# A four-layer graph network in one planned program: another start for graphs 0 to 2, and half-wise normalisation in the first and last graph

## The chip, the cores and the metric

One NeuronCore of one Trainium2 chip runs the whole program. The metric is the device time of one execution in microseconds (us). Engines: PE multiplies matrices (PEld is its weight load, which overlaps), DVE works on vectors, ACT evaluates functions, POOL does reductions over partitions and issues the adjacency loads, SP issues the other DMAs. Each engine runs its own queue strictly in order; an instruction whose input is not there holds up everything behind it on that engine.

## The reference

Sixteen graphs of 1024 nodes with 128 features pass four layers. Each layer adds its input and normalises each row (mean 0, variance 1):

```python
x = _layernorm(x + gat(x, adj, W0, a0))            # layer 0: one head, relu
x = _layernorm(x + gat8(x, adj, adj, W1, a1))      # layer 1: 8 heads of 16, elu
x = _layernorm(x + rgcn(x, adj, rel_w, self_w, ..))# layer 2: mean over neighbours, own layernorm, relu
x = _layernorm(x + attn4(x, adj, W3))              # layer 3: 4 heads of 32, masked softmax
```

The adjacency matrix holds 0 and 1 (about 3% ones). In layers 0 and 1 the logit of a pair is leaky_relu(s_i + t_j), so its exponential factors: per source j and head the kernel needs max(R_i, q_j) times the mask, where R is a row over all target nodes, the same on all 128 partitions, and q_j one number per partition.

## The kernel before

**Tiling.** 1024 nodes are 8 blocks of 128. Work is in transposed form: source nodes on partitions, target nodes along the row. In the line numbers of the profile:

- `before0` (L597): loads adjacency `m` (eight 128x1024 tiles, cast to fp8 by POOL's DMA, L605), the transposed features `xT` (L621), multiplies them with W0 joined with the two attention vectors and a mean column (`products`, L393), copies the result to `hd` and `mean` (L629, L636), takes the maximum of the target terms (L643, then all-reduce L416), and makes r, q and the scaling of hd (L654 to L681). The row R0 over all partitions: for graph 0 by eight products of r, broadcast, with the identity (L585, into PSUM); for the others by a transpose (L498), a copy (L500), a write of 8x128 to DRAM (L503) and a load that repeats it on all partitions (L672).
- `layer0` (L687): per half of the targets and per j one DVE instruction of 128x512 makes z (L697), PE adds four products of 129 columns to two accumulators (L709); then L741, L730, the residual L750 and the normalisation.
- `before1`, `layer1` (L755, L839): as layer 0, with eight heads: 64 DVE instructions of 128x1024 a graph (L849), each with eight narrow PE products (L857). For graph 0 the first four rows come by products with the identity (L585, copied by ACT, L810), all others through DRAM (L814).
- `last1` (L915), `layer2` (L937): elu and residual (L920, L924, L929), sums (L423), normalisation; then products with the weights, split in three bf16 parts (L952 to L975), 192 PE products with the mask (L989), means (L1010), normalisation, gamma and beta (L1026, L1033), relu and residual (L1040), sums, normalisation.
- `before3`, `layer3` (L1050, L1119 on): heads, their norms (L1104) and the bound `low` (L1111); then per half and j: the squared mask gap by ACT (L1129), scores by PE (L1139 for the mask, L1150), the exponential by ACT (L1221), values and totals by PE (L1165, or L1176 and L1187 in the last two graphs, where DVE adds pairs first, L1243), and the tail L1255 to L1288. The last graph is normalised half by half at this point already.
- `layernorm` (L427): DVE offsets (L438 or L442), eight ACT squares with sums (L448), Ln and Exp (L461, L466), five small DVE instructions (L470 to L480), eight ACT applications (L486). Its argument `half` restricts it to four blocks.

**What sets the order.** Every operation is a `step` with an engine, an expected duration, a due time and what it reads and writes. `Plan.run` (L168) emits steps one at a time: for each engine it finds the earliest possible start by its own expected times and the free buffers, and among the steps within a small `WINDOW` of it the one with the earliest due time. So the due times (the many constants added to `due` and `at`) decide the order within each engine, and the program that results is fixed. `plan.user` gives users of a scarce pool turns. The waits in the program come from the instructions' real operands, not from what a step is said to read. After graph 2 or 3 the order is periodic: layer 3 of one graph runs beside layers 0, 1 and 2 of the next ones.

**Buffers that matter here:** 9 tiles z, 7 tiles R, two accumulators acc1, two PSUM work areas wk, one tile x0, and two each of x1, x2, x3 (layer outputs).

Of the kernel before, what the change touches and what calls it, by code (L numbers as in the profile page):

```python
# [76 lines left out]
class Plan:  # L77
# [8 lines left out]
    SAME = 43.42  # L86
    WINDOW = {"DVE": 0.32, "ACT": 0.56, "POOL": 24.74, "SP": 1.21, "PE": 0.04}
    URGENT = 87.13
# [79 lines left out]
    def run(self):  # L168
# [18 lines left out]
        while left:  # L187
# [17 lines left out]
            for buf in s.bufs:  # L205
                if buf.place is None:
                    buf.place = min((p for p in self.places[buf.pool] if p.holder is None), key=lambda p: p.free)
                    buf.place.holder = buf
                    if buf.pool in self.turns:
                        self.turns[buf.pool].remove(buf)  # L210
# [23 lines left out]
def tile_binary(  # L234
# [62 lines left out]
    LATER1 = 126.77  # L297
    LATER3 = -19.68
    LATERX = 258.97
# [43 lines left out]
    places("x1", 2, [P, NB, P])  # L343
    places("x2", 2, [P, NB, P])
    places("x3", 2, [P, NB, P])
# [40 lines left out]
    def products(xT, w, due, into, us, floor=0.0):  # L386
# [14 lines left out]
        step("PE", us, due - 42.13, emit, [xT, w], [out], holds=[into], floor=floor)  # L401
        return out, lambda: out.t.rearrange("p (k c) -> p k c", c=SLOT)[:, :, :cols]

    def turned(x_nat, chunk, due):
# [3 lines left out]
            "PE", 0.44, due - 52.2, lambda: transposes(pt.t, [x_nat.t[:, chunk * HB + k, :] for k in range(HB)]),  # L408
            [(x_nat, chunk), xT, identity], [pt],
        )  # L410
        step("ACT", 0.47, due + 19.59, lambda: nc.scalar.copy(xT.t, pt.t[:, :HALF]), [pt], [xT])
        return xT

    def over_partitions(v, op, shape, due, op_us=None):
        got = little(f"all{shape[1]}", shape)
        step("POOL", 0.6 if op_us is None else op_us, due - 256.91, lambda: nc.gpsimd.partition_all_reduce(got.t, v.t, P, op), [v, heated], [got], lag=0.6)  # L416
        return got

    def sums(y, half, tot, due):
# [3 lines left out]
            "DVE", 0.62, due - 13.18, lambda: nc.vector.tensor_reduce(tot.t[:, ks], y.t[:, ks, :], AX.X, ALU.add),  # L423
# [3 lines left out]
    def layernorm(y, tot, due, rest=None, half=None):  # L427
# [16 lines left out]
        step("DVE", 0.1, due - 236.47, minus_mean, [tot_of, rest] if rest else [tot_of], [off])  # L444
# [7 lines left out]
        for pair in pairs:  # L452
            step(
                "ACT", 1.05, due + pair - 6.55, lambda pair=pair: square(pair), [off, (y, pair // 2)], [(squared, pair), junk]
            )
# [4 lines left out]
            "ACT", 0.17, due - 65.07,  # L460
# [4 lines left out]
            "ACT", 0.17, due - 217.77,  # L465
# [3 lines left out]
            "DVE", 0.1, due - 138.7,  # L469
# [12 lines left out]
        step("DVE", 0.35, due - 474.69, newton, [about, var, off], [rstd, shift])  # L482
# [7 lines left out]
        for pair in pairs:  # L490
            step("ACT", 0.77, due + pair - 6.15, lambda pair=pair: apply(pair), [shift, rstd], [(y, pair // 2)])

    def rows_everywhere(r, flat, count, due):
# [4 lines left out]
            "PE", 0.2, due + 269.89, lambda: nc.tensor.transpose(pt.t[: count * NB, :P], flat(r.t), ident), [r, rT, identity], [pt]  # L498
        )
        step("ACT", 0.2, due - 282.01, lambda: nc.scalar.copy(rT.t[: count * NB, :], pt.t[: count * NB, :P]), [pt], [rT])  # L500
        step(
            "SP", 0.5, due - 721.27,
# [7 lines left out]
    def load(due, into, out, in_, part=None):  # L510
        step("SP", 0.45, due - 48.89, lambda: nc.sync.dma_start(out=out(), in_=in_), [], [(into, part)], lag=3.0)

    def constants(due):
        none = Buf("z", "none")
        step("DVE", 0.2, due - 932.32, lambda: nc.vector.memset(none.t[:, :P], 0.0), [], [none])
        for n, (out_, in_) in enumerate(
# [7 lines left out]
                "ACT", 0.1, due - 1208.47,  # L524
                lambda out_=out_, in_=in_: nc.scalar.dma_start(out=out_(), in_=in_()),
                [none] if n == 0 else [square_of] if n == 2 else [], [square_of] if n < 2 else [identity], lag=2.5,
            )
            if n == 0:

                def table():  # L530
                    nc.scalar.preload_act_table_set("natural_log_exp_and_others")
                    nc.scalar.activation(warm, warm, AF.Exp)

                step("ACT", 1.5, due - 840, table, [], [heated])
# [1414 lines left out]
```

## Time and profile before

| | us |
|---|---|
| median of the runs (2182.18 to 2188.67) | 2186.32 |
| the profiled execution | 2186.08 |
| its span | 2184.2 |
| first z of layer 0 (L697) / of layer 1 (L849) | 24.67 / 67.75 |
| graph 0's norms (L1104) / first scores (L1139) | 234.9 / 240.8 |
| last layer 1 sums copied (L887), then `low` of graph 15 (L1111) | 2022.8, 2112.2 |
| last exponential (L1221) ends / last apply (L486) starts | 2167.0 / 2177.0 |

In the profile a group is given as line, engine, operation, output <- inputs; "idle before <- X" is time that the engine stood still ahead of it and what ended that. PE busy is the union of its matmuls as modelled; the granted clock is TensorE's, as a share of full speed. A trace counts a product of f32 operands as two matmuls (x64 rows for 32 products). The page gives busy shares of PE 94%, DVE 89%, ACT 81% over the span.

### The profile page before, as it was taken

The numbers are of one execution on the slowest core, as the hardware profiler recorded it, in microseconds if no ns is written. First come the engines' busy times: TensorE is split into PE (matmuls) and PEld (weight loads), VectorE is DVE, ScalarE is ACT, GpSimd is POOL, SyncE is SP. The second block draws the span as 40 slices with busy tenths as digits, with TensorE's granted clock in tenths as the row PEclk, the third lists the DMA queues.
The fourth block names the chain that finished last, engine by engine and source line by source line (L and its number), as shares of the span: only waits on it lengthen the run. The fifth ranks groups of instructions, "written<-read, shape, count | busy, mean of one in ns | idle before, by whom it ended". The sixth has DMA issues, their size and how long they took to land.

```text
span 2184.2 us, 55248 instructions
## 1 busy us (share of the span) xinstructions
PE 2046.5 (94%) x23344; PEld 982.0 (45%) x23344; DVE 1945.6 (89%) x2883; ACT 1761.7 (81%) x4360; POOL 109.8 (5%) x185
## 2 busy tenths in 40 slices
PE   6757999999999999999999999999999999999877
PEld 5414445453544545354454435345443635442422
DVE  5799999999999999999999999999999999999444
ACT  3414769889797979979797997979799797979987
POOL 1000000000000000000000000000000000000000
PEclk9888999999999999999999999999999999999989
DMA  7140220412323041232204122220413222020000
GB/s 114 49 98 20 65 60 15 101 38 86 43 79 57 18 100 34 86 43 93 44 18 101 33 91 38 93 43 18 101 33 91 38 91 38 2 78 11 11 2 22
DMA packets 81282, 119.97 MB, mean 55 GB/s; under 512 B 7560, under 2 KB 59136, under 8 KB 81024
## 3 DMA queue, kind: packets, MB, share of 16 engines
q1 hardware_dynamic: 62160, 99.43, 13.7%
q0 software_dynamic: 18432, 16.79, 9.5%
q8 instruction: 184, 3.01, 0.6%
q14 instruction: 74, 0.61, 0.1%
q10 hardware_dynamic: 432, 0.13, 0.0%
HBM read 157.61 MB, written 9.04 MB: 76 GB/s over the span
## 4 chain that ended last, share of the span: by engine, by line
PE 47%; DVE 29%; issue 15%; ACT 5%; DMA 2%; POOL 1%; POOLq 0%; SPq 0%; DVEq 0%; ACTq 0%
DVE z L849 18%; PE acc L709 10%; PE acc L1165 10%; PE acc L857 9%; PE wk L1150 6%; PE wk L384 3%; PE wk L393 3%; PE wk L1139 2%; POOL all L416 1%; PE wk L1062 1%; DMA R<-rows 1%; DVE tot L423 1%; PE acc L1176 1%; DVE rest L957 1%; DVE x L964 1%
## 5 line engine op out<-in xcount | busy, mean ns | idle before, releaser
L849 DVE SCALAR_TENSOR_TENSOR z<-R,q,m 128x1024 f32<-128x1024 f32 x1024 | 1248.2, 1278 | 23.0 <-PE acc L857 20.7
L857 PE MATMUL acc<-z,hh 128*32 128x512 f32 x4096 | 516.7, 613 | 59.4 <-DVE z L849 57.0
L1221 ACT ACTIVATE z<-wk,low 128x1024 f32<-128x1024 f32 x448 | 477.8, 1108 | 29.8 <-PE wk L1150 27.5
L1165 PE MATMUL acc<-z,hh 128*32 128x512 f32 x1792 | 454.3, 598 | 1.7 <-ACT z L1221 1.7
L1165 PE MATMUL acc<-z,ones 128*32 128x512 f32 x1792 | 454.3, 598 | 0.0
L448 ACT ACTIVATE junk<-x,off 128x128 f32<-128x128 f32 x640 | 257.1, 402 | 42.8 <-DVE off L442 26.7
L1150 PE MATMUL wk<-whT,turn 32*64 32x512 f32 x3952 | 287.0, 615 | 0.0
L857 PEld LDWEIGHTS acc<-z,hh 128*32 128x32 f32 x4096 | 117.5, 111 | 367.0 <-issue 226.8
L486 ACT ACTIVATE x<-x,shift,rstd 128x128 f32<-128x128 f32 x640 | 264.6, 487 | 6.8 <-DVE shift L480 6.6
L709 PE MATMUL acc<-hd,z 128*128 128x129 f32 x2048 | 252.3, 279 | 8.2 <-DVE z L697 4.3
L709 PEld LDWEIGHTS acc<-hd,z 128*128 128x128 f32 x2048 | 240.7, 194 | 38.4 <-DVE z L697 16.7
L1165 PEld LDWEIGHTS acc<-z,hh 128*32 128x32 f32 x1792 | 89.6, 109 | 213.2 <-issue 181.7
L697 DVE SCALAR_TENSOR_TENSOR z<-R,q,m 128x512 f32<-128x512 f32 x240 | 165.9, 744 | 22.0 <-DMA R<-rows 22.0
L989 PEld LDWEIGHTS <-m 128*128 128x128 fp8e5 x3072 | 178.4, 98 | 14.4 <-issue 14.4
L989 PE MATMUL wk<-y,m 128*128 128x128 bf16 (+1 forms) x2976 | 175.7, 220 | 0.9 <-DVE y L975 0.9
L1129 ACT ACTIVATE gap<-m,neg_one 128x512 bf16<-128x512 fp8e5 x240 | 171.4, 716 | 0.0
L1139 PEld LDWEIGHTS <-far 32*32 32x32 bf16 x4096 | 37.1, 87 | 217.0 <-issue 214.3
L448 ACT ACTIVATION_READ_ACCUMULATOR junk<-x,off 128x1 f32 x640 | 120.8, 189 | 0.0
L1165 PEld LDWEIGHTS acc<-z,ones 128*32 128x32 f32 x1792 | 89.5, 109 | 53.1 <-issue 53.1
L1139 PE MATMUL wk<-gap,far 32*32 32x512 bf16 x3784 | 106.7, 386 | 5.7 <-ACT R L1221 5.4
L605 POOL DMA_DIRECT2D m<-in_adj_dram x128 | 68.4, 539 | 723.6 <-ACT gap L1129 698.3
L660 ACT ACTIVATE r<-r 128x8 f32<-128x8 f32 x16 | 3.3, 208 | 119.7 <-DVE r L654 119.7
(158 smaller groups left out, 2120.7 us busy)
## 6 DMA issues: line engine op xcount, KB each, us to landing
R<-rows SPq DMA_DIRECT2D x139, 512.0 KB
m<-in_adj_dram POOLq DMA_DIRECT2D x128, 128.0 KB, 5.3
xT<-in_xT_dram SPq DMA_DIRECT2D x32, 256.0 KB
x<-in_x_dram SPq DMA_DIRECT2D x16, 512.0 KB
out_dram<-x SPq DMA_DIRECT2D x15, 512.0 KB
rows<-rT SPq DMA_DIRECT2D x16, 32.0 KB
out_dram<-x SPq DMA_DIRECT2D x2, 256.0 KB
z<-in_L_gnn_a_dram SPq DMA_DIRECT2D x2, 128.0 KB
```

What stands on the lines that cost most here:

```text
L448: nc.scalar.activation(junk.t, y.t[:, k, :], AF.Square, bias=off.t[:, k : k + 1], accum_out=squared.t[:, k : k + 1])
L486: nc.scalar.activation(y.t[:, k, :], y.t[:, k, :], AF.Identity, bias=shift.t[:, k : k + 1], scale=rstd.t[:, k : k + 1])
L697: nc.vector.scalar_tensor_tensor(z.t[:, (j % 2) * HALF : (j % 2 + 1) * HALF], in0=R0.t[:, cols], scalar=q.t[:, j : j + 1], in1=m[j].t[:, c ...
L709: nc.tensor.matmul(av[k // 2].t.rearrange("p (k c) -> p k c", k=2)[:, k % 2, : P + 1], lhsT=z.t[:, at : at + P], rhs=hd.t[:, j, : P + 1], ...
L849: nc.vector.scalar_tensor_tensor(z.t, in0=G["R"][h].t, scalar=q.t[:, j, h : h + 1], in1=m[j].t, op0=ALU.max, op1=ALU.mult)
L857: nc.tensor.matmul(av[half].t[32 * c : 32 * c + 32, :], lhsT=hh.t[:, j, at : at + 32], rhs=zs[c].t[:, half * HALF : (half + 1) * HALF], st ...
L989: nc.tensor.matmul(ps.t[:, k * SLOT : k * SLOT + part.stop - part.start], lhsT=m[j].t[:, rows_i], rhs=y2.t[:, j, part], start=j == 0 and n ...
L1129: nc.scalar.activation(gap.t, m[j].t if b == B - 1 else m[j].t[:, cols], AF.Square, bias=neg_one, accum_out=squares[:, at : at + 1], satur ...
L1139: nc.tensor.matmul(sc[h // 2].t[c * 32 : (c + 1) * 32, (h % 2) * HALF : (h % 2 + 1) * HALF], lhsT=far[rows_r, rows_r], rhs=gap.t[rows_r, c ...
L1150: nc.tensor.matmul(sc[h // 2].t[r * 64 : (r + 1) * 64, (h % 2) * HALF : (h % 2 + 1) * HALF], lhsT=turns[j // HB].t[rows_h, j % HB * P + r ...
L1165: nc.tensor.matmul(av[g].t[at : at + 32, :], lhsT=lhsT, rhs=z.t[:, h, :], start=j == 0, stop=j == NB - 1,)
L1221: lambda g=g, sc=sc, zs=zs: nc.scalar.activation(zs[g].t.rearrange("p h n -> p (h n)"), sc[g].t, AF.Exp, bias=low.t, scale=S3),
```

## The change

Seven things, and all due times and planner constants are set anew (not shown; they reorder every queue).

1. Graph 0's row R0 no longer comes by r and the identity. PE multiplies W0's source vector, repeated over 128 columns, with xT: the sum s_i appears on all partitions at once, in PSUM. DVE adds the maximum and clamps (two halves), ACT takes the exponential. R0 is a tile of pool R.
2. The features of graphs 0 and 1 are loaded first (graph 1's into tiles of pool xTc). The three small DMAs that build the identity go from ACT's queue to SP's, behind these; ACT's table load comes first on ACT.
3. Adjacency loads: graph 1's are said to follow the identity (before: graph 0's maximum), graph 2's to follow graph 1's row R0.
4. Graph 2's layer 0 has a start of 50 instead of two periods, so that it stands with graphs 0 and 1 in the order.
5. `last1` and `layer2` of the first and last graph are done in two halves, normalisations, gamma, beta, relu and sums too. Each layernorm in halves has the same ACT squares and applications but two sets of the small instructions.
6. x1, x2 and x3 share one pool of five tiles (before: two each).
7. Graph 0's layer 1 is planned with all four rows of a group there, and the first tiles of pool R have turns.

```diff
+        if b == 0:
+            straight = Buf("wk", "straight")
...
+            xT = Buf("xTc" if b == 1 else "xT0", "xT0")
...
+            if b == 0:
+                step(
+                    "PE", 0.9, -700 + chunk + 225.08,
+                    lambda xT=xT, chunk=chunk: nc.tensor.matmul(
+                        straight.t[:, chunk * HALF : (chunk + 1) * HALF],
+                        lhsT=w0c.t[:, P : P + 1].to_broadcast([P, P]),
+                        rhs=xT.t, start=True, stop=True,
+                    ),
+                    [xT, w0c], [(straight, chunk)],
+                )
...
-            R0 = G["R0"] = Buf("wk", "R0_0")
+            R0 = G["R0"] = Buf("R", "R0_0")
             for half in range(2):
-                step("PE", ..., row_by_products(lambda: r.t, R0, range(half * HB, half * HB + HB)), [r, identity], [(R0, half)])
+                step("DVE", 0.7, ..., tensor_scalar(R0.t[:, cols], straight.t[:, cols], most.t, 0.0, ALU.add, ALU.max), ...)
+                step("ACT", 0.6, ..., activation(R0.t[:, cols], R0.t[:, cols], AF.Exp, scale=-(1.0 - SLOPE)), ...)
...
-        if b == 1:
-            masks(range(NB), due + 40, [G["after"]])
+        if b in (1, 2):
+            masks(range(NB), due + 40, [identity if b == 1 else graphs[1]["R0"]])
...
+    def portions(b):
+        if b in (0, B - 1):
+            return [(half, slice(half * HB, (half + 1) * HB)) for half in range(2)]
+        return [(None, slice(0, NB))]
...
-        layernorm(o, tot, due + 60.03)
+        for part, ks in portions(b):
+            layernorm(o, tot, due + 60.86, half=part)
...
-    places("x1", 2, [P, NB, P])
-    places("x2", 2, [P, NB, P])
-    places("x3", 2, [P, NB, P])
+    places("x", 5, [P, NB, P])
...
-        at0 = 25 if b == 1 else at
+        at0 = 25 if b == 1 else 50 if b == 2 else at
```

## The prediction

> **What bounds the kernel now.** I read the page first (busy shares, then the 40 slices of 54.6 us), then one table of busy time by stage, then the order of time at both ends.
>
> ```profile
> PE 2046.5 (94%) x23344; PEld 982.0 (45%) x23344; DVE 1945.6 (89%) x2883; ACT 1761.7 (81%) x4360; POOL 109.8 (5%) x185
> ...
> PE   6757999999999999999999999999999999999877
> ...
> DVE  5799999999999999999999999999999999999444
> ACT  3414769889797979979797997979799797979987
> ```
>
> From slice 5 to slice 37 PE is full. The stage table gives 592.67 busy us of 600 for 400 to 1000 us, with DVE at 562.39. The middle is PE-bound with 1.2% idle, and the change leaves PE's work as it is. What can move is PE's idle time at the ends: about 76 us before the first layer 3 (240.9), and 21 us between 2018 and 2166.
>
> ```profile
> 24.67:67.75 43.08, 37.63 (x310) 36.65 (x311) 27.80 (x56) 21.25 (x83) 1.84 (x4) 0.96 0.41 64
> 67.75:156.40 88.65, 54.39 (x356) 18.55 (x358) 85.37 (x82) 21.31 (x60) 6.70 (x10) 0.83 0.37 90
> 156.40:234.90 78.50, 58.03 (x502) 39.42 (x501) 73.64 (x114) 42.71 (x129) 0.00 (x0) 0.87 0.05 14
> ...
> 2018.00:2107.00 89.00, 68.22 (x794) 29.75 (x786) 39.72 (x84) 81.64 (x188) 0.82 (x1) 0.92 0.03 7
> 2107.00:2166.00 59.00, 58.52 (x812) 15.21 (x810) 29.33 (x42) 51.73 (x83) 1.17 (x1) 0.94 0.04 11
> ```
>
> Columns: window, length, then busy us of PE, PEld, DVE, ACT, POOL, granted clock, DMA share, GB/s. Five stages, each with its own bound: layer 0 of graphs 0 and 1 is PE's (37.6 of 43); layer 1 is DVE's (85.4 of 88.7, PE waiting); graph 0's layer 2 and the way to its layer 3 are DVE's again; the last graph's chain is ACT's (81.6 of 89); its layer 3 is PE's (58.5 of 59).
>
> **Start, step 1: layer 0 begins earlier.**
>
> ```profile
> 8.71 3.40 PE L393 MATMUL wk<-w0c,xT 128*128 128x131 f32 x16 [8.71 <-DMA xT<-in_xT_dram]
> ...
> 17.10 0.23 DVE L535 TENSOR_SCALAR far<-b_ident 128x128 bf16<-128x128 f32 x1 [9.93 <-DMA b_ident<-square]
> 18.10 0.15 DVE L643 TENSOR_REDUCE top<-hd 128x1 f32<-128x8 f32 x1
> ...
> 22.30 0.22 ACT L660 ACTIVATE r<-r 128x8 f32<-128x8 f32 x1
> ...
> 24.67 6.68 DVE L697 SCALAR_TENSOR_TENSOR z<-wk,q,m 128x512 f32<-128x512 f32 x10 [1.20 <-PE wk L585]
> ```
>
> The projection ends at 12.1, but the maximum (L643) sits on DVE behind L535, which waits for the identity until 17.10; then r waits on ACT behind graph 1's copies (22.30), and L585 builds the row with the identity. In the changed kernel far is later and the row comes from the features: two products of 512 columns (0.57 us each by row L1062, times 1.65, as L393 takes 0.213 us here against 0.13 later): 14.0. The maximum is out at 13.7 (copies 0.8, L643 and all-reduce 0.6), two DVE passes of 0.67 end at 15.3, ACT's two exponentials at 15.9. q then stands on ACT behind the copy of graph 1's mean, about 16.2. First z at **16.4 instead of 24.67**: 8.3 earlier. PE's first L709 comes at 18.4 instead of 25.47, since graph 0's scaling on ACT now stands behind four copies for graph 1.
>
> Queues it is moved past. The identity's three DMAs go from ACT's queue to SP's, behind four feature loads: start 3.5 instead of 1.35, so landing about 19.3 instead of 17.1. Behind them on SP wait the constants, x0 and graph 1's row. On PE the transpose of graph 1's r, third in layer 0, waits for the identity: 0 to 1.5 us. Graph 1's row landed at 38.17; now its values are ready at 20.5, SP reaches them near 23, and 3.9 of bounce and the 8.3 that L672 took from issue (29.85) bring it to about 36; PE's first use is at 38. Adj: "gated" only orders POOL's queue, the chip waits for nothing new there; graph 2's eight loads go behind graph 1's. Twelve loads and the features kept DMA full from 18.6 to 38.8, some 1.6 us a load, so eight more end near 51, before their use at 57.
>
> **Step 2: graph 2's layer 0 moves in.** PE's order now has three graphs before the first layer 1: 192 products of L709 at 7.41/32 = 0.232 us make 44.5; 32 of L585 7.2; the projections of graph 2 2.1 and w1c's for two graphs 4.1; transposes 2.3; the rest 0.6. That is 60.8, and at the present share of gaps in this stage (5.5 in 43) 69.3. PE starts layer 1 at 18.4+69.3 = **87.7**; it was at about 72. DVE, nine z buffers ahead, has by then done 48 z of layer 0 and nine of layer 1.
>
> **Step 3: DVE from there to graph 0's norms (L1104).** By its order it has 96 z of layer 1 left (1.205 us pitch, 115.7) and 30 us of small work, 145.6; it idles 6 of 167 us in these two stages now, so 151.6: norms at 239.3, before 234.9. In front of it lie, against before, 2 z (2.4), graph 2's head work (2.1) and graph 0's halves: four more sets of L470 to L480 (0.85 each, 3.4) and small change. PE, however, has done 4.1 us more by then (graph 2's transposes 1.0, w1c products 2.1, two z 1.0). Start: 4.4 later, 4.1 less to do: **nil**. The ends: with layer 0 as dense as its best half (7.41 busy of 7.55) norms come at 234, gain 5; with another 4 us of waits at 243, loss 4. I take a gain of 1, near the middle. The 8.3 us are not lost, but graph 2's layer 0 only changes places: it filled 12.6 us of DVE at 212 to 236 before.
>
> **A rule against step 2.** PE's granted clock in the layer 1 stage is 0.83 with PE busy 54.39 of 88.65, so at full clock 45.1. The Trainium skill (TensorE: Matmul & The Clock Gate, "The HAM clock gate") says that an idle window of about 3.4 us drops the array to half clock. If the thinner stage ran wholly at half clock, its 45.1 would be 90, over DVE's 85.4, and PE would bind there: about 5 us worse; the trace shows 0.83 at 61% load, so I do not add it.
>
> **Tail.**
>
> ```profile
> 2057.11 0.69 DVE L975 TENSOR_TENSOR y<-rest,y 128x512 bf16<-128x512 f32 x1 [0.28 <-ACT y L970]
> ...
> 2082.67 1.22 DVE L1026 TENSOR_TENSOR x<-x,b_gamma_bc 128x1024 f32<-128x1024 f32 x1 [4.31 <-ACT x L486]
> ...
> 2112.21 0.15 DVE L1111 TENSOR_SCALAR low<-all 128x1 f32<-128x1 f32 x1 [0.24 <-POOL all L416]
> ```
>
> DVE idles 4.31 us while ACT normalises all eight blocks, although four would do to go on. From the copies of the last layer 1 sums (2022.76) to low, the point from which graph 15's scores may start, it is 89.5 us. In the new ACT order that stretch loses one 0.71 us and five 1.14 us adjacency squares (moved behind it) and gains two exponentials (1.0 each) and three Ln/Exp pairs (0.5 each): 2.9 us less. Of the 7.4 us in which ACT idles I count 4.4 as filled: 2.46 before the xTc copy at 2048.8, then 1.22, 0.6 and part of the small ones, as the second half's squares stand there now. Low is **7.3 earlier**. The deferred squares less the exponentials, 4.4 us, go into the next stage, where ACT has 59-51.7 = 7.3 free but PE has none: I charge 1.5 (0 to 4.4). Tail: gain **5.8**; ends 0 (nothing filled, all repaid in waits) and 9.
>
> Splitting costs: five DVE passes of 128x1024 (1.22) become ten of 128x512 (0.69), 0.8 us by durations, nil by pitch (1.25 against 0.61). VectorE: DVE Perf Modes, in its errata section, names a fixed cost for each instruction and advises tiles of at least 512 elements; the halves have 512, and the rows bear out the fixed cost (0.16 us of 0.69).
>
> **Middle.** PE's order from graph 3 on has the same products, 836 changes of kind instead of 828. Nil taken; ends -3 and +12 (below).
>
> **Sum**, against the profiled execution's 2186.08 (span 2184.2 and 1.9 outside; the median is 2186.32): 2186.1-1.0-5.8 = **2179.3**.
>
> **Rivals.** *Start pays too:* the three layer 0s pack without gaps, as projections stand between halves; for it, 1.93 us of drain ahead of each half (34.81, 45.79) that other products can fill; against, the drain between halves of graph 0 has nothing to fill it. Start -5, tail -6: 2175. *Given back:* ACT, 92% busy in 2120 to 2166, cannot absorb the squares, and the start is 243: +4-3 = about 2187, no change. *Slower:* PE waits for DVE in every period. Layer 1 of each graph starts about 4 us earlier in PE's order than before, and DVE comes to each graph's norms 4 us later against its z. Now PE's weight loads wait for L849 37.5 us in 400 to 1900, 3.1 a graph, in gaps that PE mostly covers. If only 0.9 us more a graph becomes bare, 13 graphs make 11.7: 2191 with the tail kept. It decides from 1 us a graph (13 against the 6.8 gained). Against: DVE has 6% free there.
>
> **Numbers.** 0.3% is 6.6 us, about what a measurement here tells from no change. Forecast 0.50 (its own range 2173 to 2185; 0.28 below 2179.8), start pays 0.18, given back 0.14, slower 0.18. Faster 0.28+0.18 = 0.46; same 0.22+0.14 = 0.36; slower 0.18. The range goes from the three good ends together (2186-5-9-3 = 2169) to just past the slower rival's 2191; what is beyond, half of that rival and little at the low end, is about 1 in 10.
>
> **What would show it.** First L697 near 16.4; PE's first layer 1 near 88; graph 0's L1104 at 234 to 243; low 82 after the last layer 1 copies, not 89.5; PE 98.8% busy in 400 to 1900. I am wrong if norms come before 230, if PE's share in the middle moves by over 0.5%, or if low is not earlier.

## The result, and the profile after

The changed kernel is slower: 2201.15 us median (2199.38 to 2208.7, 6 runs) against 2184.25 us (2179.26 to 2188.67, 6 runs) of the kernel before, ratio 1.0085 with a 95% interval of 1.0062 to 1.0108. 2179.3 was forecast, with a range from 2169 to just past 2191. The profiled execution took 2200.45 us, span 2198.6, 14.4 more than before. In the changed kernel's lines products of layer 0 are L726 (DVE) and L738 (PE), those of layer 1 L881 and L889, the norms L1147.

The first view is the page's busy shares and slices (55.0 us each).

```profile
PE 2054.1 (93%) x23332; PEld 979.3 (45%) x23332; DVE 1955.6 (89%) x2930; ACT 1753.1 (80%) x4375; POOL 102.8 (5%) x185
...
PE   5856699999999999999999999999999999999877
...
DVE  3798999999999999999999999999999999999554
```

The middle is as full as it was. The loss stands in the first slices: PE shows 5, 8, 5, 6, 6 where it showed 6, 7, 5, 7, 9. The stages up to the norms (the first boundary is here PE's first matmul of layer 1, in the table of before the first product of layer 1; window, length, busy us of PE, PEld, DVE, ACT, POOL, granted clock, DMA share, GB/s):

```profile
14.84:102.60 87.76, 65.20 (x519) 63.17 (x517) 53.23 (x101) 47.88 (x172) 10.21 (x19) 0.90 0.50 85
102.60:184.00 81.40, 49.61 (x290) 12.18 (x291) 74.97 (x74) 12.79 (x40) 0.82 (x1) 0.75 0.22 72
184.00:263.30 79.30, 53.14 (x429) 28.01 (x429) 68.98 (x122) 42.14 (x126) 1.25 (x1) 0.81 0.10 32
```

Layer 0 of three graphs takes 87.8 us, and PE is idle for 22.6 of them; before, up to the same boundary (24.67 to 75.07), two graphs took 50.4, and PE was idle for 8.5. In the two stages behind it DVE, the bound, stands still for 6.4 and 10.3 us; it was 3.3 and 4.9. Where it stands during layer 0, by DVE's order of time first in the changed kernel, then before (start, length, what ended the idle time ahead):

```profile
14.84 1.41 DVE L726 SCALAR_TENSOR_TENSOR z<-R,q,m 128x512 f32<-128x512 f32 x2 [0.81 <-ACT q L704]
...
47.91 4.07 DVE L726 SCALAR_TENSOR_TENSOR z<-R,q,m 128x512 f32<-128x512 f32 x6 [15.02 <-DMA R<-rows]
```

```profile
38.17 4.73 DVE L697 SCALAR_TENSOR_TENSOR z<-R,q,m 128x512 f32<-128x512 f32 x7 [0.47 <-DMA R<-rows]
```

The first product comes at 14.84, 9.8 us earlier than before. At one place it turns into a lag of 9.7: DVE waits 15.0 us for graph 1's row, which is there at 47.9 and not at 38.2. SP's order of time shows its two transfers, first in the changed kernel, then before:

```profile
16.47 0.64 SPq L714 DMA_DIRECT2D x<-in_x_dram  x1
17.15 3.89 SPq L515 DMA_DIRECT2D b_gamma_bc<-in_L_gnn_ln_gamma_dram  x1
...
26.18 1.31 SPq L507 DMA_DIRECT2D rows<-rT  x1
41.49 0.35 SPq L699 DMA_DIRECT2D R<-rows  x1
```

```profile
25.47 0.35 SPq L503 DMA_DIRECT2D rows<-rT  x1
29.85 0.34 SPq L672 DMA_DIRECT2D R<-rows  x1
```

SP begins to issue the 4 KB write of the row at 26.18, and the read that needs it leaves at 41.49: 15.3 us, where it was 4.4 before. The 512 KB read then takes 6.4.

A ledger of VectorE up to graph 0's norms puts the loss together (busy time by stage, start times of the norms):

| us | before | after | difference |
|---|---|---|---|
| first matmul of layer 1 | 75.1 | 102.6 | +27.5 |
| graph 0's norms | 234.9 | 263.3 | +28.4 |
| DVE busy up to there | 190.2 | 200.3 | +10.1 |
| DVE idle up to there | 44.7 | 63.0 | +18.3 |
| norms of graph 0 to graph 13 | 1642.8 | 1637.8 | -5.0 |
| to graph 14, to graph 15 | 125.6, 106.1 | 120.8, 102.0 | -8.9 |
| to the end | 74.8 | 74.7 | -0.1 |

18.3 of the 28.4 us is new idle time, 10.1 is more work ahead of the norms. About half of that work has moved there (two products of layer 1, 2.7; one scaling of `hh`, 1.2; a residual and a set of small instructions, 1.5). The rest is new: three more sets of small instructions and the shorter passes of graph 0's halves, and the two passes that make its row. 48 products of layer 0 stand ahead of the norms in both kernels.

The last three rows give 14.0 us back, so that 14.4 are left. PE, which bounds the middle, says it for the whole span: it is idle for 12.5 us more up to the norms and 5.7 less behind them, and its busy time grows by 7.6 (2046.5 to 2054.1) with 12 matmul records fewer; its clock in the first stages is lower (0.90, 0.75 and 0.81, where the table of before has 0.96, 0.83 and 0.87).

### The profile page after: what moved, and what is told of

It is laid out like the page before. It is cut to its first block, busy times and chain, and to the rows that moved or that the text cites. A ratio compares the mean times of both kernels' runs of the same rounds, so it can differ in the third digit from the quotient of the medians.

```text
span 2198.6 us, 55390 instructions
## 1 busy us (share of the span) xinstructions
PE 2054.1 (93%) x23332; PEld 979.3 (45%) x23332; DVE 1955.6 (89%) x2930; ACT 1753.1 (80%) x4375; POOL 102.8 (5%) x185
## 4 chain that ended last, share of the span: by engine, by line
PE 53%; DVE 33%; ACT 9%; issue 3%; DMA 1%; SPq 1%; POOL 0%; DVEq 0%; ACTq 0%; POOLq 0%
DVE z L881 24%; PE acc L889 10%; PE acc L738 10%; PE acc L1208 8%; PE wk L1033 7%; PE wk L1193 6%; PE wk L382 3%; PE wk L391 3%; ACT junk L446 2%; PE wk L1182 2%; ACT z L1264 1%; ACT R L1264 1%; PE wk L1105 1%; DVE tot L421 1%; DVE x L971 1%
## 5 line engine op out<-in xcount | busy, mean ns | idle before, releaser
L881 DVE SCALAR_TENSOR_TENSOR z<-R,q,m 128x1024 f32<-128x1024 f32 x1024 | 1246.2, 1279 | 19.8 <-PE acc L889 16.1
L889 PE MATMUL acc<-z,hh 128*32 128x512 f32 x4096 | 521.2, 619 | 55.4 <-DVE z L881 52.9
L1264 ACT ACTIVATE z<-wk,low 128x1024 f32<-128x1024 f32 x448 | 475.3, 1105 | 39.3 <-PE wk L1193 30.9
L1208 PE MATMUL acc<-z,ones 128*32 128x512 f32 x1792 | 440.7, 597 | 0.0
L446 ACT ACTIVATE junk<-x,off 128x128 f32<-128x128 f32 x640 | 256.7, 401 | 69.5 <-DVE off L440 54.1
L889 PEld LDWEIGHTS acc<-z,hh 128*32 128x32 f32 x4096 | 107.1, 111 | 362.1 <-issue 206.0
L738 PE MATMUL acc<-hd,z 128*128 128x129 f32 x2048 | 252.1, 279 | 8.6 <-ACT x L759 7.1
L738 PEld LDWEIGHTS acc<-hd,z 128*128 128x128 f32 x2048 | 241.1, 194 | 37.3 <-ACT x L759 18.8
L726 DVE SCALAR_TENSOR_TENSOR z<-R,q,m 128x512 f32<-128x512 f32 x256 | 177.3, 745 | 16.2 <-DMA R<-rows 15.0
L1208 PEld LDWEIGHTS acc<-z,ones 128*32 128x32 f32 x1792 | 96.7, 109 | 122.2 <-issue 122.2
```

Of the source, the lines that this page charges most:

```text
L446: nc.scalar.activation(junk.t, y.t[:, k, :], AF.Square, bias=off.t[:, k : k + 1], accum_out=squared.t[:, k : k + 1])
L726: nc.vector.scalar_tensor_tensor(z.t[:, (j % 2) * HALF : (j % 2 + 1) * HALF], in0=R0.t[:, cols], scalar=q.t[:, j : j + 1], in1=m[j].t[:, c ...
L738: nc.tensor.matmul(av[k // 2].t.rearrange("p (k c) -> p k c", k=2)[:, k % 2, : P + 1], lhsT=z.t[:, at : at + P], rhs=hd.t[:, j, : P + 1], ...
L881: nc.vector.scalar_tensor_tensor(z.t, in0=G["R"][h].t, scalar=q.t[:, j, h : h + 1], in1=m[j].t, op0=ALU.max, op1=ALU.mult)
L889: nc.tensor.matmul(av[half].t[32 * c : 32 * c + 32, :], lhsT=hh.t[:, j, at : at + 32], rhs=zs[c].t[:, half * HALF : (half + 1) * HALF], st ...
L1208: nc.tensor.matmul(av[g].t[at : at + 32, :], lhsT=lhsT, rhs=z.t[:, h, :], start=j == 0, stop=j == NB - 1,)
```

## The experiments

Four theories at first. **T1**: graph 2's eight adjacency loads, which wait for nothing on the chip, keep the transfer engines full, and SP's transfers behind graph 0's features and graph 1's row suffer. **T2**: the row stands behind the constants in SP's own order. **T3**: graph 2's early layer 0 costs by itself, through DVE's waits behind the start. **T4**: SP's new order and the halves cost as much as graph 2. T5 and T6 came later. No run has the number E11. Each round of runs had the kernel before beside it (medians 2183.6 to 2185.1 us), to which the ratio is taken. "Row" is the first product of graph 1, "layer 1" PE's first matmul of it, idle that of DVE up to the norms; these are from one profiled execution each, and the same program's start differs by some us from one to the next (last section).

| run | median us | ratio to before, 95% | row | layer 1 | norms | idle |
|---|---|---|---|---|---|---|
| before | 2184.25 | | 38.2 | 75.1 | 234.9 | 44.7 |
| after | 2201.15 | 1.0085 (1.0062 to 1.0108) | 47.9 | 102.6 | 263.3 | 63.0 |
| E1 hold | 2196.06 | 1.0049 (1.0031 to 1.0066) | 40.1 | 98.1 | 258.7 | 58.4 |
| E2 write from ACT | 2199.97 | 1.0073 (1.0055 to 1.0091) | 46.9 | 101.6 | 257.9 | 57.7 |
| E3 both | 2192.69 | 1.0040 (1.0027 to 1.0053) | 37.2 | 91.9 | 250.9 | 50.7 |
| E4 row by products | 2203.55 | 1.0085 (1.0066 to 1.0104) | 47.1 | 104.6 | 263.2 | 64.1 |
| E5 graph 2 in its period | 2203.00 | 1.0088 (1.0074 to 1.0102) | 38.7 | 78.9 | 236.8 | 58.0 |
| E6 last halves only | 2211.67 | 1.0125 (1.0109 to 1.0141) | 49.5 | 105.8 | 269.4 | 69.3 |
| E7 no halves | 2219.98 | 1.0167 (1.0150 to 1.0183) | 49.5 | 105.8 | 269.4 | 69.1 |
| E8 as E5, last halves only | 2225.59 | 1.0197 (1.0180 to 1.0214) | 40.8 | 79.5 | 246.2 | 62.7 |
| E9 before, last halves | 2182.08 | 0.9984 (0.9972 to 0.9995) | 38.7 | 76.2 | 235.3 | 45.3 |
| E10 before, straight row | 2185.14 | 1.0003 (0.9994 to 1.0012) | 39.6 | 76.8 | 232.8 | 42.0 |
| E12 PE filled | 2204.41 | 1.0092 (1.0079 to 1.0106) | 49.0 | 107.0 | 266.5 | 66.3 |
| E13 as E3, square from ACT | 2194.98 | 1.0049 (1.0035 to 1.0062) | 36.8 | 96.3 | 256.7 | 56.4 |
| E14 before, both parts | 2180.42 | 0.9986 (0.9976 to 0.9996) | 39.3 | 75.3 | 231.4 | 40.4 |
| E15 constants behind | 2202.86 | 1.0086 (1.0071 to 1.0101) | 50.1 | 105.1 | 264.3 | 64.1 |
| E16 as E15, hold | 2196.65 | 1.0061 (1.0046 to 1.0076) | 38.4 | 96.0 | 255.0 | 54.6 |
| E17 as E3, DVE reordered | 2197.04 | 1.0056 (1.0041 to 1.0070) | 40.0 | 96.4 | 252.8 | 50.5 |

**E1, the loads of graph 2 held.**

```diff
+        def load_mask(m, j):
+            if b == 2 and j == 0:
+                nc.gpsimd.tensor_copy(gate, graphs[1]["R0"].t[:, :1])
+            nc.gpsimd.dma_start(out=m.t, in_=adjT[b, j * P : (j + 1) * P, :])
```

> The changed kernel with one instruction more: GpSimd copies one column of graph 1's row into a scratch column before it issues the first of graph 2's eight adjacency loads, so that these loads really wait for the row. Theory T1 (the loads of graph 2 fill the transfer engines, and the row's 4 KB write stands behind them): the write lands 4 to 8 us after its issue at 26.2 instead of 15.3, graph 1's row is there near 38 to 41 instead of 47.9, PE is 7 to 10 us further at the end of layer 0, and the time is 2191 to 2196. Theory T2 (the write stands behind SP's own earlier transfers, 512 KB of features and the constant rows, in SP's own queue): the write still lands at 38 to 42 and the row at 45 to 48; graph 2's loads start 20 us later, near 47, so the time is 2201 to 2208. Theory T3 (putting graph 2's layer 0 early is what costs, wherever its loads stand): 2199 to 2203.

**E2, the row's write from ScalarE's queue.**

```diff
-            lambda: nc.sync.dma_start(
+            lambda: queue.dma_start(          # nc.scalar for graph 1's row
```

> The changed kernel with graph 1's 4 KB write of the row issued on ScalarE's queue, right behind the copy that makes it, instead of on SP's behind the constants. T2 (order in SP's own queue): issue near 21.3, landing within 4 to 6 us (3.9 is what such a write took in the kernel before), the row's read issued near 26 and landed near 34; graph 1's layer 0 starts about 13 us earlier, time 2186 to 2191. T1 (transfer engines full of graph 2's loads): the write still takes about 15 us from its issue, lands near 36, row near 42, time 2194 to 2198. T3: row early, time still 2198 to 2202.

**E3, both.**

> Both edits: the write on ScalarE's queue, and graph 2's loads held until graph 1's row has landed. T1 and T2 agree that the row comes at 31 to 35; T1 expects this to be better than the write alone by 3 us or more (2188 to 2192 against 2194 to 2198), T2 expects the hold to bring nothing more or to cost 0 to 4 us, as graph 2's loads then end near 50 instead of 47 (2186 to 2193). T3: 2198 to 2202.

**E4, the row without any transfer.**

```diff
-            kept = rows_everywhere(r, lambda t: t, 1, due - 745.69)
+                step("PE", 1.9, due - 390.41, row_by_products(lambda: r.t, pt), [r, identity], [pt])
+                step("ACT", 1.0, due - 1229.99, lambda: nc.scalar.copy(R0.t, pt.t), [pt], [R0])
```

> The changed kernel with graph 1's row made without any transfer: eight matmuls against the identity into PSUM and one copy by ScalarE, as layer 1 of graph 0 makes four of its rows; the 4 KB write and the 512 KB read are gone, the loads of graph 2 stand as they stood. T1 and T2 alike: the row is there near 25 to 28, graph 1's layer 0 follows graph 0's without the 15 us wait of VectorE, time 2184 to 2190. T3 (early graph 2 costs by itself, through work of VectorE ahead of graph 0's layer 1): the wait is gone, yet graph 0's first norms are still later than 250 and the time is 2194 to 2201.

E1 came out at the end of T1's range (2196.06, the row at 40.1), but for SP's arrival. The write is issued at 32.8 and not at 26.2, and the read can follow 3.2 us later:

```profile
32.78 0.35 SPq L508 DMA_DIRECT2D rows<-rT  x1
36.02 0.35 SPq L705 DMA_DIRECT2D R<-rows  x1
```

E2's time of 2199.97 lies in T3's range and cannot be told from the changed kernel's. E4, in which the row does not pass through a transfer at all, gained nothing either and is slower than every theory had it. DVE's order of time in E4 says why:

```profile
45.85 0.69 DVE L784 TENSOR_TENSOR x<-x,x 128x512 f32<-128x512 f32 x1 [16.61 <-DMA x<-in_x_dram]
```

With the row out of the way DVE stands just as long one instruction earlier, for graph 0's features, whose load SP had issued at 19.3. So it is not the row alone, but what stands in SP's queue while the adjacency loads run. In E3 both arrive in time. DVE's and GpSimd's order of time:

```profile
33.85 0.69 DVE L785 TENSOR_TENSOR x<-x,x 128x512 f32<-128x512 f32 x1 [1.73 <-DMA x<-in_x_dram]
...
37.15 4.06 DVE L732 SCALAR_TENSOR_TENSOR z<-R,q,m 128x512 f32<-128x512 f32 x6 [0.62 <-DMA R<-rows]
...
37.32 4.23 POOL L607 DMA_DIRECT2D m<-in_adj_dram  x8
```

The features are there 10 us sooner than in E2, the row 10.8 sooner than in the changed kernel, and graph 2's loads, now from 37.3, are still early enough. Half of the loss is gone (1.0085 to 1.0040).

E2's median did not separate T1 from T2, since its row's read still stood on SP, whose issue of one constant row took 11.0 us. Its packets say more. Transfers by queue in E2 between 29.6 and 30.4 us (packets, MB, share of the 16 engines' time; q0 carries GpSimd's loads, q1 SP's transfers, q10 ScalarE's):

```profile
q0 software_dynamic: 86, 0.08, 102.4%
q1 hardware_dynamic: 88, 0.01, 15.4%
q10 hardware_dynamic: 16, 0.00, 3.7%
```

The 16 packets of q10 are the write, issued at 26.3. So beside the same loads, but on a queue of its own, it was through within 4 us, and T1's 15 us did not come. The read left at 40.1, when SP had issued its constants. What is slow is SP's queue, and it is slow while the loads run. The same view from 28 to 40 us, first of the changed kernel, then of E1:

```profile
q0 software_dynamic: 1241, 1.13, 99.8%
q1 hardware_dynamic: 982, 0.33, 16.5%
```

```profile
q1 hardware_dynamic: 3193, 1.82, 57.2%
q0 software_dynamic: 316, 0.28, 24.9%
```

With graph 2's loads held, SP's queue moves 1.82 MB in these 12 us instead of 0.33.

**E15 and E16, five constants issued behind graph 1's row, without and with the hold of E1.**

```diff
-        step("SP", 0.45, due + 375.16, lambda: nc.sync.dma_start(out=out(), in_=in_), [], [(into, part)], lag=3.0)
+        step("SP", 0.45, due + 375.16, lambda: held.append(issue) if hold else issue(), [], [(into, part)], lag=3.0)
...
+                    [issue() for issue in held] if b == 1 else None,      # behind the read of the row
```

> The changed kernel with five constants (both layer-norm rows, self_w, w3, a1) issued on SP behind graph 1's row instead of ahead of it; graph 2's loads still free to start. In E2 SP stood 11.0 us in issuing the first of these rows, with the row's read behind it. T2 (order on SP): the write is issued at 21 to 23, the row lands by 38 and the time is 2190 to 2196. T1 (the transfer engines are full with graph 2's loads, whatever stands first on SP): the row lands at 43 or later, since its write and read and the 512 KB of graph 0's features still share the engines with them, time 2197 to 2202.

> Both the constants behind graph 1's row and graph 2's loads held until that row has landed. If order and fullness are each a part, the row lands at 32 to 36, the first matmul of layer 1 comes at 88 to 92 and the time is 2189 to 2194, no better than the hold with ScalarE's queue (2192.7) by more than 3 us: what is left over the kernel before (2184.8) is then no longer a matter of transfers. If transfers are still the bound, it is below 2188.

SP's order of time in E15:

```profile
21.27 4.04 SPq L722 DMA_DIRECT2D x<-in_x_dram  x1
26.81 9.22 SPq L507 DMA_DIRECT2D rows<-rT  x1
46.23 0.36 SPq L705 DMA_DIRECT2D R<-rows  x1
```

No constant stands between features and row any more, and the row still comes at 50.1: the features stand ahead of it, and to issue the 4 KB write takes SP 9.2 us. From 28 to 40 us of E15 the queues show

```profile
q0 software_dynamic: 1251, 1.14, 102.2%
q1 hardware_dynamic: 1253, 0.17, 16.6%
```

As many packets of one queue go through as of the other, but one of the loads carries 0.9 KB on average and one of SP's 0.14. 1021 of SP's are of 64 bytes: they are the load of `w1c`, 1024 pieces of that size, issued at 20.6, ahead of the features. So the order of the constants is not the cause by itself (T2 as E15 puts it). With the hold the row comes at 38.4 and the time is 2196.65, a smaller gain than either branch had for E16. The three pairs that differ by the hold (changed kernel and E1, E2 and E3, E15 and E16) gain 5 to 7 us. The row is late for two reasons together, what SP has queued ahead of it and loads that leave this queue little.

**E5 and E8, graph 2 back in its own period; E8 with the first graph whole.**

```diff
-        at0 = 25 if b == 1 else 50 if b == 2 else at
+        at0 = 25 if b == 1 else at
```

with its loads, floors and lags as those of later graphs.

> The changed kernel with graph 2's layer 0 put back into its own period: its loads, features and row no longer stand ahead of graph 0's layer 1; the row of graph 0 straight from the features, the first issue of two graphs' features, SP's order of the constants and the halves of the first and last graph stay. Theory T1 (as E1 and E3 let it stand: graph 2's loads hold up SP's transfers, graph 0's features and graph 1's row) and T3 (graph 2's early layer 0 leaves later waits of VectorE uncovered) agree here: features of graph 0 by 34, row of graph 1 by 34 to 38, first matmul of layer 1 at 70 to 76 (before 75.1, changed 102.6), and with the last graph's 4.7 us the time is 2172 to 2183. Theory T4 (the new order of the constants on SP and the halves cost as much as graph 2): first matmul of layer 1 near 80 to 85, time 2188 to 2196.

> As the run before it (graph 2 in its own period), and only the last graph normalised by halves, the first graph whole. If halving the first graph costs (14 more small operations of VectorE and its in-order waits in the stretch up to the first norms), this is 1 to 4 us faster than its neighbour, 2169 to 2180; if halving there shortens the chain, it is 1 to 4 us slower.

E5's times lie outside both ranges, and layer 1 starts at 78.9, between T1's 70 to 76 and T4's 80 to 85. Its norms at 236.8 look like those of before, but DVE has 11.4 us less work ahead of them (178.8 busy) and stands idle for 58.0 us, 13.3 more than before. Graphs 1 and 2 then follow at distances of 138.1 and 134.5 us, where the kernel before has 124.4 and 126.5; E8 has 144.1 and 146.0, and is 22.6 us slower than E5 where 1 to 4 were expected either way. 16.4 us of E5's idle time lie behind the first matmul of layer 1, as in the changed kernel, although graph 2 is not early. That speaks against T3. But the due times of the changed kernel were set for graph 2 early, and the planner makes another order of these edits throughout. So neither run prices graph 2's place, and T4 is neither shown nor refuted.

**E6 and E7, halves for the last graph only, and for none.**

```diff
-        if b in (0, B - 1):
+        if b == B - 1:          # E7: if b in ():
```

> The changed kernel, with graph 2 early as it is, and the first graph normalised whole; the last graph by halves. Theory T5 (halves of graph 0 leave VectorE waiting: 16.8 us idle between the first matmul of layer 1 and the first norms, 8.1 before): idle falls to 10 to 13 us, time 2194 to 2198. T1 and T3: the waits stay, as they come from graph 2's work no longer standing there, 2198 to 2204.

> The changed kernel with no halves at all. Against its neighbour that halves the last graph: from the last copies of layer 1 to graph 15's bound 89 us instead of 84 (before 89.2, changed 84.2), so 3 to 5 us slower than that neighbour. If the halves of the last graph were worth nothing on the chip, the same time as that neighbour within 1.5 us.

T5, that halves of the first graph cost, is not borne out: without them this order is 10.5 us slower by the medians, and DVE's idle time behind the start rises to 19.7 us instead of falling (norms 6.1 later, of which 3.2 were there at layer 1 already; the next period 128.4 for 124.1). Here too the due times were set for the halves. In both E6 and E7 DVE waits 4.0 us at graph 0's means, which it does not in the changed kernel. The halves of the last graph are worth 8.3 us by the medians, where 3 to 5 were expected, 5.5 of it between the norms of graphs 14 and 15 (109.4 against 103.9).

**E9, E10, E14: single parts put into the kernel before.** E9 halves its last graph (`portions` with `b == B - 1`, as in the diff above). E10 takes graph 0's row straight from the features. E14 has both, and the steps that need the identity or late constants no longer ahead of layer 0:

```diff
-        step("DVE", 0.2, due - 74.81, ..., [identity], [farther])
+        step("DVE", 0.2, due - 74.81, ..., [identity], [farther], floor=38.0)
...                                    # two more steps get the same floor
```

> The kernel before, with one part of the change: the last graph's layers 1 and 2 normalised by halves; up to the last graph every engine's order is that of the kernel before. If the halves are worth what the changed kernel's tail shows (84.2 us from the last copies of layer 1 to graph 15's bound, 89.2 before) and what the pair E6 and E7 shows (8 us with the end), the time is 2176 to 2180; if they pay only in the order of the changed kernel, 2183 to 2186.

> The kernel before, with one part of the change: graph 0's row straight from the features (two matmuls with a broadcast column, VectorE and ScalarE on PSUM) instead of eight products against the identity; two graphs' loads, graph 2 in its period, identity on ScalarE's queue as before. If the early row is worth its lead, the first product of layer 0 is at 14 to 17 instead of 24.7, the first matmul of layer 1 at 68 to 72 instead of 75.1, and the time 2177 to 2181. If the lead is lost at the next transfer (graph 1's row, which lands at 38.2 before), layer 1 starts at 74 to 76 and the time is 2183 to 2187.

> The kernel before with two parts of the change, and the place where the first of them was lost mended: graph 0's row straight from the features, the steps of VectorE and PE that need the identity or late constants no longer ahead of layer 0 (in E10 VectorE waited 9.9 us for the identity in front of the first product), and the last graph by halves. If graph 2's place is the whole reason that the changed kernel is slow, and its other parts are sound: first product at 14 to 17, first matmul of layer 1 at 70 to 75, time 2174 to 2180. If a lead at the first product is lost at graph 1's row whatever is done: layer 1 at 75 to 78, time 2180 to 2185.

E9 gains 3.0 us by the medians, between its two forecasts, but its profiled execution, the slowest of the twelve, shows no shorter way from the last copies to `low` (90.8 us), so where it gains is open. E10 gains nothing: DVE waits 9.9 us for the identity, then for graph 1's copies, and the first product is at 24.0 still. In E14 that wait is gone, and DVE waits 8.4 and 6.7 us for graph 1's copies in the same place, since graph 1's features are late: first product 24.8, which neither branch had. So the straight row alone brings no earlier product here; with both graphs' features first, as in the changed kernel, it does. E9 and E14 are the two versions under the kernel before, by less than 0.2%.

**E12, PE filled in graph 0's layer 1.** The stage's granted clock was 0.75; could the cold PE be what T3's waits are made of?

```diff
+                if b == 0 and j < NB - 1:
+                    for c in range(G1):      # the same four products again, into a free bank
+                        nc.tensor.matmul(acc3s[0][32 * c : 32 * c + 32, :], ..., start=True, stop=True)
```

> The changed kernel, with PE's share in graph 0's layer 1 doubled by matmuls of no use: each group of four is run once more into a PSUM bank that is free at that time, except in the last block of a group of heads. If PE's low granted clock in that stage (0.57 from 140 to 160, where sixteen matmuls take 3.3 to 3.6 us instead of 1.92) is what makes VectorE wait 7.5 us in three places for PE's transposes behind the last matmuls, the clock rises above 0.9, the three waits fall to 3 us or less and the time to 2194 to 2198. If the waits come from the order alone (nothing of VectorE stands between the last product and the reciprocal that follows), they stay within 1.5 us, and the time is 2199 to 2206.

Twenty us of the changed kernel, then the same of E12, in the table by stage:

```profile
140.00:160.00 20.00, 11.45 (x56) 2.08 (x60) 20.00 (x18) 0.00 (x0) 0.00 (x0) 0.57 0.00 1
```

```profile
140.00:160.00 20.00, 12.91 (x100) 3.67 (x96) 17.17 (x16) 1.07 (x2) 0.00 (x0) 0.83 0.20 69
```

Sixteen matmuls that took 3.4 to 3.6 us there mostly take 1.9 to 2.1, the granted clock is 1.00 in 120 to 140 and 160 to 180, and of DVE's three waits the two in graph 0's layer 1 fall from 5.2 us to 2.8; the third, 2.3 us, stands in graph 1's layer 1, which has no filling, and stays. From layer 1's first matmul to the norms it is only 1.2 us less (159.5 against 160.7), because PE, now with twice the work, makes DVE wait 1.7 us more elsewhere; the run began that stage 4.4 us late besides. About half of the two waits is the cold PE's, and little of the time is.

**E13, the identity sooner.** T6: the rest of E3's late start is the identity, whose chain the change put on SP behind the features.

```diff
+            if n == 0:
+                nc.scalar.dma_start(out=square_of.t, in_=none.t[:, :P])
+                nc.scalar.dma_start(out=square_of.t...[:: P + 1]..., in_=ones[:, :1])
```

> The kernel with the hold and the write on ScalarE's queue (E3: identity there at 22.9, VectorE idle 9.0 us at the first reciprocal because PE stands at the transposition of graph 1's row), and the two writes that build the identity's square on ScalarE's queue too, ahead of SP's features. Theory T6 (the identity's chain, which the change put on SP behind 1 MB of features, is the rest of the late start): the identity lands at 15 to 18, the row of graph 1 at 31 to 34 instead of 36.5, the first matmul of layer 1 at 86 to 89 instead of 91.9, time 2186 to 2190. T3 (what is left of E3's 7.6 us over the kernel before is the waits of VectorE after the start): the start gains less than 2 us or the gain is lost again, 2191 to 2195.

The identity was used at 18.3, 4.6 us sooner, and the row's read left at 25.3 for 32.0, but it landed at 36.8 like E3's: it now ran beside graph 1's loads. PE, out of work, stood 3.2 us for graph 2's features. The table by stage shows the same 6.8 us of both kernels, E3 first:

```profile
42.60:49.40 6.80, 6.42 (x58) 6.36 (x58) 6.41 (x19) 6.48 (x31) 0.69 (x1) 1.00 1.10 107
```

```profile
42.60:49.40 6.80, 6.71 (x35) 6.69 (x36) 6.04 (x15) 4.29 (x20) 0.69 (x1) 0.56 1.09 112
```

PE is as busy, at a granted clock of 0.56 in place of 1.00, and finishes 35 matmuls in place of 58: a run of 32 of layer 0 takes 6.65 us where E3 needs 3.84. Layer 1 starts 4.4 us later than in E3, and the time is no better (2194.98): T6 is refuted as the rest of the loss.

**E17, DVE's order behind the start, on E3.** Two lags in the planner for graph 0, so that three products stand ahead of the first reciprocal behind a head group, and one more ahead of layer 2's first sum:

```diff
-                    [av[half]], [(oT, half)], holds=[lent] if b == B - 1 else [],
+                    [av[half]], [(oT, half)], holds=[lent] if b == B - 1 else [], lag=3.0 if b == 0 else None,
...
-                [ps], [(y2, chunk)],
+                [ps], [(y2, chunk)], lag=4.5 if b == 0 and chunk == 0 else None,
```

> The kernel with the hold and the write on ScalarE's queue (E3: VectorE idle 50.7 us up to graph 0's norms, 44.7 in the kernel before; 15.1 of it behind the start, 8.1 before), with more of VectorE's work put ahead of the places where it waits there: the planner reckons with 3 us after the last copies of each group of heads of graph 0 and with 4.5 after one copy of its layer 2, so that three products of the next group stand ahead of the first reciprocal and one more ahead of layer 2's first sum. If what is left of the loss is VectorE standing, in its order, at PE's and ScalarE's small chains, its idle time up to the norms falls to 45 to 48 and the time to 2187 to 2190. If the idle time is only moved to other places, 2191 to 2195.

The two waits go (2.8 us to 0.6, 4.2 to nothing), and DVE's idle time behind the start falls from 15.1 to 10.3 us. But this run's start was 4.5 us later, its row was there at 40.0, and the next period took 128.4 us instead of 124.0: the idle time moved to other places, as the second branch had it, though 2197.04 lies above that branch too. E3 has the lowest median of the mended kernels.

## Why the prediction was wrong, step by step

**The step that failed is in step 1: graph 1's row**, "3.9 of bounce and the 8.3 that L672 took from issue (29.85) bring it to about 36". The bounce (the write, until the read could leave) took 15.3 us, and the row was there at 47.9: 26.2 + 15.3 + 6.4 where the prediction had 23 + 3.9 + 8.3. Both prices were taken from the trace of before, in which eight loads fewer ran at that time; the same paragraph had the loads ("the chip waits for nothing new there; graph 2's eight loads go behind graph 1's") and asked only when they would be there for their own use, not what they would do to a transfer beside them. It also took SP's arrival at the row as 23, and it was 26.2: one constant row of 64 KB held SP for 3.9 us. E1, E3 and E16 show the cause by holding the loads. E2, E4 and E15 show that the row's way or the constants alone do not mend it, since the rest of SP's queue is as late. The Trainium skill (DMA: Bandwidth & Descriptors, "Issuing engines are not separate DMA queues") says that transfers started by the scalar, sync or gpsimd engine run on the same 16 DMA engines and interleave. The traces agree: in E15, 1251 packets of GpSimd's loads and 1253 of SP's transfers went through in the same 12 us. But a small write on a queue of its own was not slow beside these loads, as E2 shows with its 4 us.

**The rest of step 1 was right.** First product 14.84 (16.4 forecast), PE's first 16.6 (18.4). The transpose of graph 1's r waited 1.97 us for the identity, just over the 0 to 1.5; in E1, E2, E3, E15 and E16 it waited 3.3 to 7.0 us and in E8 9.4, so that bound was too tight.

**Step 2** had layer 1 at 87.7, 69.3 us behind PE's first product; it came at 102.6, 86.0 behind it. PE was busy for 64.9 of these (60.8 forecast, at a clock of 0.90) and idle for 21.0 (8.5). Of the 14.9 us, 10.7 are gone in E3 (91.9), in one execution each. The rest I put down to the identity and PE's clock from the waits and the clock in the profile, and E13 shows that taking away the first alone brings nothing. The "about 72" for the kernel before was misread as well: its first matmul of layer 1 comes at 75.1.

**Step 3** had the stretch up to the norms at 151.6 us with 6 us idle; it took 160.7, and 16.8 of it idle (8.1 before). "It idles 6 of 167 us in these two stages now" misread the prediction's own table, which gives 88.65 - 85.37 and 78.50 - 73.64, or 8.1, and the figure was carried over to another order: the waits at the reciprocals behind the head groups (7.5 us, 1.7 before) and at layer 2's first sum (4.2 us, 1.5 before) had no term. E17 moved these waits and the time did not follow, so what they cost is open. "Nil" for the start thus became 28.4 us at the norms, and what lies ahead is not repaid at once but at the end, as the ledger shows.

**The rule against step 2** was not added, and that was half right. The clock in the two stages fell to 0.75 and 0.81 (0.83 and 0.87 before). E12, at a clock of 0.96 in the layer 1 stage, takes 2.4 us of waits away and 1.2 us of time, not the 5 us that the rule would have made; PE did not come to bind. In E13 a wait of 3.2 us ahead of the projection, and 2.3 us behind it, go with 0.56. The Trainium skill (TensorE: Matmul & The Clock Gate, "The HAM clock gate") names an idle window of about 3.4 us for the fall to half clock. The wait is a little under that, and no run here varies it alone.

**The tail was right in kind, and smaller.** From the last copies to `low` 84.5 us (82 forecast, 89.5 before), so 5.0 earlier and not 7.3; 0.7 repaid (1.5). By terms: ScalarE had 3.5 us less work in it (2.9 forecast) and 1.3 us less idle time (4.4). ScalarE is still the bound; DVE waits for it longer, in one piece:

```profile
2088.42 0.68 DVE L1075 TENSOR_TENSOR x<-x,b_gamma_bc 128x512 f32<-128x512 f32 x1
...
2106.39 0.69 DVE L1075 TENSOR_TENSOR x<-x,b_gamma_bc 128x512 f32<-128x512 f32 x1 [9.96 <-ACT x L484]
```

The first half is through 18 us ahead of the second, where all of it waited for all eight blocks before. E6 against E7 gives 8.6 us for the same stretch. In the order of before E14 gives 2.5 and E9 nothing, so the size depends on the order.

**The middle.** "Nil" was 5.0 us in favour over 13 periods, some 0.4 in each, from a cause that no run shows; PE's share in 400 to 1900 rose from 98.8 to 99.2%. The rival that stood for slower, PE waiting for DVE in every period, did not happen. About half of the loss came from a mechanism that had no rival and no price: a transfer made late by other transfers, with the bounds of the start at -5 and +4.

**What stays open.** E3 is 1.0040 (7.6 us by the medians) over the kernel before, and this half of the loss is not explained. DVE's ledger gives 6.0 us more idle time up to the norms, all of it behind the start, but E17 took 4.8 us of it away and the time did not follow. Starts of E3, E13, E16 and E17 also differ among themselves by 4 us (91.9 to 96.4); that this comes from when transfers land and whether PE goes cold is argued, not shown. A row whose write and read both leave SP, or a load of `w1c` in longer pieces, was not tried. Whether graph 2's early layer 0 could pay in an order planned for real landing times was not tried.

## What to carry to other kernels

Before loads are brought forward, look at the stretch in which the DMA row of the profile shows 9, and list every small transfer with a chain behind it that falls in them: its price there is not the one that the old trace shows. Look also at what is queued ahead of it on its own queue, and in how small packets. An order in the issuing engine's program is no order on the transfer engines; if a load must not run ahead of something, let it read what it has to wait for. Work moved from a PE-bound middle into the start shortens nothing unless it fills idle time there; count busy and idle time of the engine that bounds the whole, up to one fixed event and behind it, before and after.

## What the runs showed of the hardware that was not expected

- The 4 KB write held up its read for 4.4 us, 15.3 us and 3.2 us (before, after, E1) by what else ran and what stood ahead of it; on ScalarE's queue in E2 it was through in 4 us. 512 KB of features issued between 18.5 and 19.3 were there at 34 to 35 with graph 2's loads held (E1, E3), and at 43.5 and 45.9 without (E2, E4). In the changed kernel's own trace they were issued at 16.5 and caused no wait at 30.2.
- Packets, not bytes, went through in equal numbers: in 12 us of E15, 1251 of the loads (1.14 MB) and 1253 of SP's queue (0.17 MB).
- Issuing stalls with the transfers: the same constant row took SP 0.4 us to issue in E14, 3.9 in the changed kernel, 6.9 and 8.9 in E3 and E1 (graph 2's loads held), 11.0 in E2 and 12.3 in E4, and the 4 KB write 9.2 in E15.
- The same program does not start alike each time: the first matmul of layer 1 came at 102.6 us in the changed kernel and at 107.0 in E12, which has the same program up to there.
